# Eight layers on one core: the last layer and the output in steps beside the scan, dt and dt x written once

## The chip, the core and the metric

The kernel runs on one core of a Trainium2 chip. The core has four engines that work side by side: PE (TensorE, the matmuls), DVE (VectorE), ACT (ScalarE) and POOL (GpSimd). SP (SyncE) issues nearly all transfers between DRAM and the on-chip memory. Each engine has its own queue of instructions and takes them strictly in order; an instruction whose input is not ready holds up everything behind it in the same queue. The on-chip memory has two parts: SBUF for data and PSUM, into which PE writes.

The metric is the time of one execution on the device in microseconds (us). The time before is the median of three runs. The profile is of one further execution of the same program.

## The reference

Eight layers, each added to its input `x` (8 sequences, 512 positions, 128 channels, float32), with a layer norm ahead of each. The first six, two attentions with their feed-forward layers, a banded attention and an expert layer, are hardly touched. The seventh is a selective scan with a gated feed-forward behind it; the eighth counts spikes. Cut to what matters:

```python
def L3_attn(x):                      # 16 heads of 8 channels, 48 states
    u  = rmsnorm(x) * norm1_w
    xh = depthwise_conv4(u) @ pw_w.T + pw_b
    dt_x, B, C = split(xh @ x_proj_w.T)              # per head
    dt = softplus(dt_x @ dt_proj_w.T + dt_proj_b)
    h  = exp(dt * A) * h + (dt * xh) * B             # for each position in turn
    y  = sum over states of h * C
    x1 = x + y @ out_proj_w.T + out_proj_b
    h2 = rmsnorm(x1) * norm2_w
    return x1 + (silu(h2 @ gate_w.T) * (h2 @ up_w.T)) @ down_w.T

def L3_ffn(x):
    y = square(relu(x @ W_fc.T)) @ W_proj.T
    mem = 0; count = 0
    for 5 steps:
        mem   = 0.9 * mem + y - (mem > 1)
        count = count + (mem > 1)
    return count / 5

x = x + L3_attn(layer_norm(x))
x = x + L3_ffn(layer_norm(x))
```

The norm of `rmsnorm` is over the 128 channels, and so is the layer norm's.

## The kernel before

The 8 sequences lie in SBUF for the whole run as `X[b]`, four row tiles of 128 positions each (C = 4, 32 row tiles in all). Three functions run one after the other: `l0_l2_attn` (the first five layers, from 0 to about 1000 us), `l2_ffn_l3_attn` (L1138: the expert layer and the scan layer) and `l3_ffn` (L1625: the last layer). After them eight transfers write `X[b]` to the output (L1664). The weights of all layers are loaded into one pool of SBUF, `const`, and stay there.

The code is written as Python loops over tiles of pools. A framework turns each tile that is used again into waits between the engines; the order of instructions on each engine is the order in which the program issues them. A pool gives each name a number of buffers (`bufs`); a tile whose buffers are all taken makes its next writer wait for the last reader. PSUM tiles named `mm` have two buffers and serve all side work of this stage; `bx` has two, `Z` one. The decays have four, `h` six, `gx` and `dr` two, `xk` three.

**Statistics.** `stats` (L199) takes mean and variance of the four tiles of a sequence on DVE. The scan layer's input is normalised from `mv3`: `rstd_of` on DVE (L1177) and POOL (L1178, a power of -0.5), then four subtract-and-multiply on DVE (L1183). The last layer's input is normalised from `mv4` with `begin` and `normalised` (L220, after a square root on ACT for all sequences at once). `flipped` transposes four tiles on PE (L228) and copies them out on ACT (L231, or L233 with a scale).

**prepare(b)** (L1273) computes what the scan of one sequence needs. It is a generator; each `yield` ends a step, 11 in all: norm (on DVE), the scale `rr` and `u` on POOL, transposition (L233), the convolution as four matmuls over shifted input with weights `wk` (L1296; `wk` is built once on POOL, L1234), a matmul that turns the rows (L1301), one for dt (L1305), ACT's abs, exp and relu, then a polynomial for log(1 + z) on POOL in 128x512 pieces (L1315 to L1325). At its end it writes `dt` to DRAM with every row 16 times (4 MB) and `du` = dt times x with every row 8 times (2 MB).

**The scan stage.** The loop runs over b (8), q (4 blocks of 32 channels), g (3 blocks of 16 states) and j (2 halves), 192 pieces. One piece is: `bx`, four matmuls of `gx` with the weights `wb` (L1588); the decay `a`, one exp on ACT with `nA` as scale (L1594); the scan on DVE over 128 x 1024 (L1599), which reads `a` from SBUF and `bx` from PSUM and writes `h`. A group is the two pieces of one (b, q, g). After both pieces of a group the program issues:

- `give()` (L1493) for the group before: 8 matmuls `Z` of `h` with `wc` (L1501), which add up over g; with the last g, `zx` = Z times `xk` on DVE (L1509), and after the last q the generator `rest(b)` joins the list `side`.
- with g = 0 the transfers `fetch` of the next block (L1466 to L1484): four for `xk`, which spread the block's 32 rows of `xh` over 128, one for `gx` (512 KB, from `du_d`), two for `dr` (1 MB together, from `dt_d`). All are issued by SP, in this order.
- with g = 2 `products` of the next block: `gx` times `xk` on POOL (L1488).
- `step(side)`: every generator in `side` goes one step on.

`prepare(b + 2)` joins `side` when the scan of b begins; `prepare(0)` and `prepare(1)` run beside the expert layer (L1421 to L1444). So the side work stands on each engine between the instructions of the scan, in this order:

```python
for g in range(G):
    for j in range(2):
        ...
    late.append((b, q, g, hs, xk))
    if len(late) > 1:
        give()
    if after[0] < NB:
        if g == 0:
            fetch(*after)
        elif g == G - 1:
            products(*after)
    step(side)
```

**rest(b)** (L1514, 9 steps, two of them empty) ends the layer of one sequence: the sum over k (L1520) and a copy (L1525), the output projection (L1530) and the add on DVE (L1531), squares on ACT (L1622), the norm (L1535 on DVE, L1536 and L1538 on POOL), the residual on POOL (L1541), the transposition, two gate matmuls with Silu (L1550, L1552), two up matmuls with a product on DVE (L1557, L1558), the down projection (L1563), the add on DVE (L1567) and the statistics `mv4`.

**The last layer** (L1625) loops over the sequences: norm on DVE, transposition, four matmuls with `f3_fc` (L1635), relu on ACT (L1636), the square on POOL (L1637), 16 matmuls with `f3_pr` (L1641), -y on ACT (L1646). Then the five spike steps on DVE, kept as n = -mem: the first count (L1648), and four times t = 0.9 n - y (L1652), the reset (L1654) and the count (L1655); at the end 0.2 times the count is added to x (L1658). All its buffers are double.

## Time and profile before

| | us |
|---|---|
| median of three runs | 2018.02 (2016.74 to 2020.12) |
| the profiled execution | 2007.65 |
| its span, first to last instruction | 2005.9 |
| first five layers | 0 to about 1000 |
| expert layer, with `prepare` of two sequences beside it | about 1000 to 1277.5 |
| scans, with the rest of each layer beside them | 1277.5 to 1865.5 |
| rest of the last sequence's scan layer | 1865.5 to about 1892 |
| last layer and output | about 1892 to 2005.9 |

Busy time in a stretch is the sum of an engine's instructions in it. PEclk is the share of the full clock that PE was granted; the mean over the span is 0.853. "Idle before" of a group is the time its engine stood still just ahead of it, and the name behind the arrow is what ended it. The groups of the last layer (line, engine, operation, out<-in, shapes, count, busy us, mean ns, idle before and its releaser), from a view of the trace by line from 1865 us to the end:

```profile
L1637 POOL TENSOR_TENSOR h<-h 128x512 f32<-128x512 f32 x32 | 46.9, 1493 | 57.8 <-ACT h L1636 57.8
L1641 PE MATMUL o<-L_ffn_W_proj,h 128*128 128x128 f32 x256 | 41.0, 312 | 16.9 <-POOL h L1637 16.9
L1635 PE MATMUL mm<-xT,L_ffn_W_fc 128*128 128x512 f32 x64 | 30.8, 618 | 0.0
L1655 DVE SCALAR_TENSOR_TENSOR cnt<-n,cnt 128x512 f32<-128x512 f32 x32 | 26.7, 834 | 0.4
L1652 DVE SCALAR_TENSOR_TENSOR t<-n,ny 128x512 f32<-128x512 f32 x24 | 21.4, 894 | 0.0
L1654 DVE SCALAR_TENSOR_TENSOR n<-n,t 128x512 f32<-128x512 f32 x24 | 19.6, 815 | 0.2
L1636 ACT ACTIVATE h<-mm 128x512 f32<-128x512 f32 x32 | 19.1, 597 | 11.7 <-PE mm L1635 11.7
```

DVE has the most to do there, with the recurrence and the counts. The transfers of the stage around the scan, from the page (out<-in, count, KB each, median us from issue to landing):

```profile
dt_d<-dt SPq DMA_DIRECT2D x8, 4096.0 KB, 13.0
dr<-dt_d SPq DMA_DIRECT2D x64, 512.0 KB, 7.9
du_d<-du SPq DMA_DIRECT2D x8, 2048.0 KB, 14.0
gx<-du_d SPq DMA_DIRECT2D x32, 512.0 KB, 6.5
xk<-xh SPq DMA_DIRECT2D x128, 64.0 KB, 6.1
```

### The profile page before, as it was taken

The page shows a single profiled execution, that of the slowest core. Times are in us where ns is not written, and L with a number is a line of the kernel's source. Part 1 is how long each engine was busy: PE and PEld are TensorE (multiplying, and loading weights), DVE is VectorE, ACT ScalarE, POOL GpSimd, SP SyncE. Part 2 cuts the span into 40 slices and gives each one's busy share as a digit, 9 for nine tenths or more (in the row PEclk, how much of TensorE's full clock was granted, in tenths as well). Part 3 has the DMA queues.
Part 4 walks back from the last instruction along what each step waited for, and adds up shares of the span by engine and source line. Part 5 has one row for each costly group of instructions (what it writes and reads, how often), then busy time and mean ns, then how long its engine had stood idle before and what let it go on. Part 6 is the DMA issues. An engine that isn't in the chain of part 4 may idle for free.

```text
span 2005.9 us, 24650 instructions
## 1 busy us (share of the span) xinstructions
PE 1661.1 (83%) x9157; PEld 688.7 (34%) x9157; DVE 1283.0 (64%) x2369; ACT 826.5 (41%) x1197; POOL 655.8 (33%) x708
## 2 busy tenths in 40 slices
PE   6978988999989775785999999698768788698774
PEld 2322333434444363554434444112112112122353
DVE  5656666566655422454565554498878779798489
ACT  4645555544534221442323343345445346345221
POOL 5544433432211204303020054516245244211152
PEclk8989989888999997776999999758778778677788
DMA  8970000000000272000000024653864855842000
GB/s 277 383 222 1 1 1 11 17 10 9 21 16 17 88 223 61 18 1 0 1 0 1 0 79 173 193 156 107 227 192 92 246 169 131 236 111 74 1 16 27
DMA packets 118345, 181.02 MB, mean 90 GB/s; under 512 B 11464, under 2 KB 43088, under 8 KB 118224
## 3 DMA queue, kind: packets, MB, share of 16 engines
q1 hardware_dynamic: 116176, 175.24, 29.4%
q0 software_dynamic: 2048, 4.20, 0.7%
q8 instruction: 72, 1.18, 0.2%
q14 instruction: 49, 0.40, 0.1%
HBM read 74.55 MB, written 96.47 MB: 85 GB/s over the span
## 4 chain that ended last, share of the span: by engine, by line
PE 24%; DVE 14%; issue 5%; DMA 4%; POOL 4%; ACT 1%; SPq 1%; DVEq 0%; POOLq 0%; ACTq 0%
DVE h L1599 5%; PE bx L1588 5%; PE mm L1432 4%; PE acc L1421 4%; DMA dr<-dt_d 3%; PE Z L1501 3%; PE sp L1443 1%; POOL h L1637 1%; DMA gx<-du_d 1%; PE o L1641 1%; DVE act L1444 1%; DVE t L1652 1%; PE mm L1520 1%; SPq L1472 1%; DVE n L1654 1%
## 5 line engine op out<-in xcount | busy, mean ns | idle before, releaser
L1599 DVE TENSOR_TENSOR_SCAN h<-a,bx 128x1024 f32<-128x1024 f32 x192 | 427.9, 2270 | 98.4 <-ACT a L1594 53.0
L1594 ACT ACTIVATE a<-dr,nA 128x1022 f32<-128x1022 f32 x192 | 216.6, 1144 | 308.4 <-DVE h L1599 191.7
L1588 PE MATMUL bx<-gx,wb 32*64 32x512 f32 x1536 | 233.8, 814 | 94.0 <-DVE h L1599 55.1
L1444 DVE TENSOR_TENSOR act<-act,sp 128x512 f32<-128x512 f32 x128 | 87.6, 686 | 128.7 <-ACT act L1436 84.1
L1488 POOL TENSOR_TENSOR gx<-gx,xk 128x1024 f32<-128x1024 f32 x32 | 75.3, 2353 | 253.5 <-DMA gx<-du_d 222.4
L1501 PE MATMUL Z<-h,wc 64*32 64x512 f32 x1536 | 147.5, 830 | 10.5 <-DVE zx L1509 10.3
L1436 ACT ACTIVATE act<-mm 128x512 f32<-128x512 f32 x128 | 76.2, 597 | 164.7 <-PE mm L1432 155.7
L1421 PE MATMUL acc<-act,L_ffn_values 128*128 128x512 f32 x256 | 132.9, 602 | 8.2 <-DVE act L1444 8.1
L1432 PE MATMUL mm<-xT,L_ffn_keys 128*128 128x512 f32 x256 | 135.3, 610 | 0.0
L1588 PEld LDWEIGHTS bx<-gx,wb 32*64 32x64 f32 x1536 | 42.2, 159 | 260.3 <-DVE h L1599 182.5
L470 DVE TENSOR_REDUCE mx<-sm 128x8 f32<-128x1024 f32 x64 | 76.2, 1212 | 46.8 <-POOL sm L466 46.8
L498 POOL TENSOR_SCALAR_AFFINE_SELECT eT<-eT 128x1024 f32<-128x1024 f32 x64 | 68.6, 1095 | 105.6 <-ACT eT L496 105.5
L466 POOL TENSOR_SCALAR_AFFINE_SELECT sm<-sm 128x1024 f32<-128x1024 f32 x64 | 69.3, 1096 | 56.7 <-ACT sm L465 56.3
L496 ACT ACTIVATE eT<-sT 128x1024 f32<-128x1024 f32 x64 | 62.0, 1020 | 57.9 <-PE sT L489 57.8
L465 ACT COPY sm<-sc 128x1024 f32<-128x1024 f32 x64 | 63.0, 1013 | 51.3 <-PE sc L459 31.6
L1178 POOL TENSOR_TENSOR rstd<-rstd,minus_half 128x4 f32<-128x4 f32 x16 | 16.5, 1036 | 192.0 <-DVE rstd L1177 191.9
L459 PE MATMUL sc<-kb,qT 32*128 32x512 f32 x256 | 58.4, 736 | 22.4 <-ACT eT L496 10.2
L321 DVE SCALAR_TENSOR_TENSOR xn<-x,mv,rstd 128x128 f32<-128x128 f32 x128 | 45.9, 409 | 44.5 <-POOL rstd L317 44.4
L1421 PEld LDWEIGHTS acc<-act,L_ffn_values 128*128 128x128 f32 x256 | 47.1, 192 | 65.2 <-issue 46.5
L489 PE MATMUL sT<-qT,kb 32*128 32x512 f32 x256 | 57.1, 692 | 14.2 <-ACT sm L465 8.3
L1432 PEld LDWEIGHTS mm<-xT,L_ffn_keys 128*128 128x128 f32 x256 | 46.2, 192 | 65.2 <-issue 52.1
L199 DVE BATCH_NORM_STATS2 bn<-x 128x6 f32<-128x128 f32 x256 | 64.2, 271 | 6.5 <-DMA x<-in_L_attn_hidden_states 5.4
(411 smaller groups left out, 3203.9 us busy)
## 6 DMA issues: line engine op xcount, KB each, us to landing
f_in<-we SPq DMA_DIRECT2D x10, 3584.0 KB, 27.2
dt_d<-dt SPq DMA_DIRECT2D x8, 4096.0 KB, 13.0
dr<-dt_d SPq DMA_DIRECT2D x64, 512.0 KB, 7.9
du_d<-du SPq DMA_DIRECT2D x8, 2048.0 KB, 14.0
gx<-du_d SPq DMA_DIRECT2D x32, 512.0 KB, 6.5
wt<-in_L_ffn_experts SPq DMA_DIRECT2D x48, 192.0 KB, 2.8
xk<-xh SPq DMA_DIRECT2D x128, 64.0 KB, 6.1
xg<-f_in SPq DMA_DIRECT2D x48, 64.0 KB, 2.6
```

The costliest lines, as they stand in the source:

```text
L466: nc.gpsimd.affine_select(out=sm, in_=sm, compare_op=ALU.is_ge, fill=-1e30, base=0, pattern=[[0, 8], [-1, P]], channel_multiplier=1,)
L470: nc.vector.tensor_reduce(mx[:, c, 2 * i : 2 * i + 2, 0:4], sm.rearrange("p (q r) k -> p q r k", q=2), AX.X, ALU.max, negate=True,)
L498: nc.gpsimd.affine_select(out=e4, in_=e4, compare_op=ALU.is_ge, fill=0.0, base=0, pattern=[[0, 8], [1, P]], channel_multiplier=-1,)
L1421: nc.tensor.matmul(acc, f2_v[:, j, :], act, start=(j == 0), stop=(j == J - 1))
L1432: nc.tensor.matmul(mm, f2_k[:, 2 * j : 2 * j + 2, :], xT, start=True, stop=True)
L1436: nc.scalar.activation(act, mm, AF.Relu)
L1444: nc.vector.tensor_tensor(act, act, sp[j % 4], ALU.mult)
L1488: nc.gpsimd.tensor_tensor(gx, gx, xk.unsqueeze(1).to_broadcast([P, 2, S]), ALU.mult)
L1501: nc.tensor.matmul(zs[q][32 * j : 32 * j + 32, i, :], wc[half, g, :], hs[j // 2][half, j % 2, :], start=(g == 0), stop=(g == G - 1),)
L1588: nc.tensor.matmul(bx[64 * i : 64 * i + 64, k, :], wb[at, g, :], gx[at, i, :], start=True, stop=True,)
L1594: nc.scalar.activation(a[:, :, 1:], dr[:, 2 * j : 2 * j + 2, 1:], AF.Exp, scale=nA[:, q, g : g + 1],)
L1599: nc.vector.tensor_tensor_scan(h.rearrange("p r t -> p (r t)"), a.rearrange("p r t -> p (r t)"), bx.rearrange("p r t -> p (r t)"), 0.0, AL ...
```

## The change

- The last layer is no longer a function of its own. A generator `spikes(b)` of 18 steps does it for one sequence, and joins `side` when `rest(b)` has taken its statistics. Its norm runs on POOL (`normal_aside`), its square on ACT, the count of spikes on POOL, in single buffers and with the PSUM tiles `mm`; it ends with the sequence's output transfer.
- `prepare` also takes its norm on POOL, splits the convolution in two halves and has 14 steps. `rest` has 13 (further steps behind the projection's add, each gate, each up and the last add), and its small scale `r2` goes from DVE to POOL.
- `dt_d` holds dt once (256 KB, written by four transfers), `du_d` holds du once (256 KB). The repetition is in the reads: `gx` comes in two transfers, `dr` in two as before, each from a source that repeats its rows. `gx` is now fetched ahead of `xk`.
- In the scan loop `give` follows the first piece of a group, `fetch` the first piece of a block, `products` the fourth; the side work takes a step after every piece. If the rows of the next sequence aren't ready at a fetch, the side work is driven on until they are.
- Weights of the first layers go to a pool `early` that is closed ahead of the expert layer.

The loads of the other small weights of the first layers move from `const` to `early` in the same way, and the helpers `inv_sqrt`, `begin`, `normalised` and `norm_flip`, which the last layer alone used, are gone.

```diff
+    first_weights = ExitStack()
+    early = first_weights.enter_context(tc.tile_pool(name="early", bufs=1))
...
-    def l2_ffn_l3_attn():
+    def l2_ffn_to_l3():
...
+            def normal_aside(b, mv, r, xn):
+                nc.gpsimd.tensor_scalar(r, mv[:, tiles(b), 1], 1e-5, None, ALU.add)
+                nc.gpsimd.tensor_tensor(r, r, half_T, ALU.pow)
+                for c in range(C):
+                    nc.gpsimd.tensor_scalar(
                         xn[:, c, :], X[b][:, c, :], mv[:, b * C + c, 0:1], r[:, c : c + 1],
                         ALU.subtract, ALU.mult,
                     )
...
-                r = rstd_of(mv3, b)
+                r = work.tile([P, C], F32, tag="rstd", name="rstd", bufs=3)
+                xn = work.tile([P, C, D], F32, tag="x1", name="x1", bufs=4)
+                normal_aside(b, mv3, r, xn)
                 rr = work.tile([P, C], F32, tag="rr", name="rr")
                 nc.gpsimd.tensor_tensor(rr, r, r, ALU.mult)
                 nc.gpsimd.tensor_tensor(rr, rr, mv3[:, tiles(b), 1], ALU.mult)
                 nc.gpsimd.tensor_scalar(rr, rr, 1e-6, None, ALU.add)
-                nc.gpsimd.tensor_tensor(rr, rr, minus_half[:, 0:C], ALU.pow)
-                xn = work.tile([P, C, D], F32, tag="x1", name="x1", bufs=4)
-                normal(b, mv3, r, xn)
+                nc.gpsimd.tensor_tensor(rr, rr, half_T, ALU.pow)
                 x1[b] = xn
...
-                mm = mm_tile()
-                for k in range(4):
-                    nc.tensor.matmul(mm, wk[:, k], up[:, k : k + S], start=(k == 0), stop=(k == 3))
                 xh = work.tile([P, S], F32, tag="xh", name="xh", bufs=3)
-                nc.scalar.activation(xh, mm, AF.Identity, bias=xb)
-                yield True
+                for h in range(0, S, S // 2):
+                    mm = mm_tile()[:, 0 : S // 2]
+                    for k in range(4):
+                        nc.tensor.matmul(
+                            mm, wk[:, k], up[:, h + k : h + k + S // 2], start=(k == 0), stop=(k == 3)
+                        )
+                    nc.scalar.activation(xh[:, h : h + S // 2], mm, AF.Identity, bias=xb)
+                    yield True
                 mm = mm_tile()
                 nc.tensor.matmul(mm, turn, xh, start=True, stop=True)
                 xt = work.tile([P, S], F32, tag="xt", name="xt", bufs=1)
                 nc.scalar.copy(xt, mm)
+                yield True
                 mm = mm_tile()
...
-                dt_d = dram.tile([P, 16, S], F32, tag="dt_d", name="dt_d", bufs=3)
-                nc.sync.dma_start(dt_d, dt.unsqueeze(1).to_broadcast([P, 16, S]))
                 du = work.tile([P, S], F32, tag="du", name="du")
                 nc.gpsimd.tensor_tensor(du, dt, xt, ALU.mult)
-                du_d = dram.tile([P, HD, S], F32, tag="du_d", name="du_d", bufs=3)
-                nc.sync.dma_start(du_d, du.unsqueeze(1).to_broadcast([P, HD, S]))
+                yield True
+                dt_d = dram.tile([2 * Q, 4, 4, S], F32, tag="dt_d", name="dt_d", bufs=3)
+                for r in range(4):
+                    nc.sync.dma_start(dt_d[:, r], dt[r :: 4])
+                du_d = dram.tile([P, S], F32, tag="du_d", name="du_d", bufs=3)
+                nc.sync.dma_start(du_d, du)
                 rows[b] = xh, dt_d, du_d
...
                     of = slice(32 * q, 32 * q + 32)
+                    gx = scan.tile([P, 2, S], F32, tag="gx", name="gx")
+                    for i in range(2):
+                        nc.sync.dma_start(
+                            gx[:, i, :],
+                            du_d[32 * q + 16 * i : 32 * q + 16 * i + 16]
+                            .unsqueeze(1).to_broadcast([16, HD, S]),
+                        )
                     xk = scan.tile([P, S], F32, tag="xk", name="xk", bufs=3)
                     for i in range(4):
                         nc.sync.dma_start(xk[32 * i : 32 * i + 32], xh[of])
-                    gx = scan.tile([P, 2, S], F32, tag="gx", name="gx")
-                    nc.sync.dma_start(
-                        gx, du_d[of].rearrange("m k t -> (m k) t").rearrange("(i p) t -> p i t", i=2)
-                    )
                     dr = scan.tile([P, 4, S], F32, tag="dr", name="dr")
                     for i in range(2):
                         nc.sync.dma_start(
                             dr[64 * i : 64 * i + 64],
-                            dt_d[32 * q + 16 * i : 32 * q + 16 * i + 16]
-                            .rearrange("m s t -> (m s) t").rearrange("(j p) t -> p j t", j=4),
+                            dt_d[2 * q + i].rearrange("r j t -> r (j t)")
+                            .unsqueeze(1).to_broadcast([4, 16, 4 * S]),
                         )
                     rows4[b, q] = xk, gx, dr
...
                     nc.vector.tensor_tensor(xn, xn, pr, ALU.add)
+                    yield True
                     square_sums(xn, ss, b, scan)
                     yield True
                     t = tiles(b)
-                    nc.vector.tensor_scalar(r2[:, t], ss[:, t], 1.0 / D, 1e-6, ALU.mult, ALU.add)
-                    nc.gpsimd.tensor_tensor(r2[:, t], r2[:, t], minus_half[:, 0:C], ALU.pow)
+                    nc.gpsimd.tensor_scalar(r2[:, t], ss[:, t], 1.0 / D, 1e-6, ALU.mult, ALU.add)
+                    nc.gpsimd.tensor_tensor(r2[:, t], r2[:, t], half_T, ALU.pow)
...
                     nc.vector.tensor_tensor(X[b], X[b], o, ALU.add)
+                    yield True
                     stats(b, mv4)
+                    side.append(spikes(b))
+                    yield True
+                def spikes(b):
+                    r = work.tile([P, C], F32, tag="rstd", name="rstd", bufs=3)
+                    xn = scan.tile([P, C, D], F32, tag="u2", name="xn3", bufs=1)
+                    normal_aside(b, mv4, r, xn)
+                    yield True
+                    xT = scan.tile([P, S], F32, tag="hT", name="hT3", bufs=1)
+                    flipped(xn, mm_four(), xT)
+                    yield True
+                    h = scan.tile([P, 4, S], F32, tag="h3", name="h3", bufs=1)
+                    for k in range(4):
+                        mm = mm_tile()
+                        nc.tensor.matmul(mm, f3_fc[:, cols(k)], xT, start=True, stop=True)
+                        nc.scalar.activation(h[:, k, :], mm, AF.Relu)
+                        nc.scalar.activation(h[:, k, :], h[:, k, :], AF.Square)
+                        yield True
+                    ny = scan.tile([P, C, D], F32, tag="ny", name="ny", bufs=1)
+                    for c in range(C):
+                        o = mm_tile()[:, 0:D]
+                        for k in range(4):
+                            nc.tensor.matmul(
+                                o, h[:, k, cols(c)], f3_pr[:, k, :], start=(k == 0), stop=(k == 3)
+                            )
+                        nc.scalar.activation(ny[:, c, :], o, AF.Copy, scale=-1.0)
+                        yield True
+                    ny = ny.rearrange("p c d -> p (c d)")
+                    cnt = scan.tile([P, S], F32, tag="cnt", name="cnt", bufs=1)
+                    nc.gpsimd.tensor_scalar(cnt, ny, -1.0, None, ALU.is_lt)
+                    n = ny
+                    for _ in range(4):
+                        t = scan.tile([P, S], F32, tag="t3", name="t3", bufs=1)
+                        nc.vector.scalar_tensor_tensor(t, n, 0.9, ny, ALU.mult, ALU.add)
+                        n2 = scan.tile([P, S], F32, tag="n3", name="n3")
+                        nc.vector.scalar_tensor_tensor(n2, n, -1.0, t, ALU.is_lt, ALU.add)
+                        n = n2
+                        yield True
+                        hit = scan.tile([P, S], F32, tag="hit", name="hit", bufs=1)
+                        nc.gpsimd.tensor_scalar(hit, n, -1.0, None, ALU.is_lt)
+                        nc.gpsimd.tensor_tensor(cnt, cnt, hit, ALU.add)
+                    yield True
+                    yield True
+                    xf = X[b].rearrange("p c d -> p (c d)")
+                    nc.vector.scalar_tensor_tensor(xf, cnt, 0.2, xf, ALU.mult, ALU.add)
+                    yield True
+                    nc.sync.dma_start(out[b].rearrange("(c p) d -> p c d", p=P), X[b])
                     yield True
...
                                 hs.append(h)
+                                if j == 0 and late:
+                                    give()
+                                if after[0] < NB and (g, j) == (0, 0):
+                                    while after[0] not in rows:
+                                        step(side)
+                                    fetch(*after)
+                                elif after[0] < NB and (g, j) == (1, 1):
+                                    products(*after)
+                                step(side)
                             late.append((b, q, g, hs, xk))
-                            if len(late) > 1:
-                                give()
-                            if after[0] < NB:
-                                if g == 0:
-                                    fetch(*after)
-                                elif g == G - 1:
-                                    products(*after)
-                            step(side)
                 give()
                 while side:
                     step(side)
-            state["mv"] = mv4
...
-    def l3_ffn():
-        with ExitStack() as es:
...
-    for layer in (l0_l2_attn, l2_ffn_l3_attn, l3_ffn):
-        layer()
-    for b in range(NB):
-        nc.sync.dma_start(out[b].rearrange("(c p) d -> p c d", p=P), X[b])
+    l0_l2_attn()
+    first_weights.close()
+    l2_ffn_to_l3()
```

## The prediction

> **What bounds the kernel now.** I first cut the span at the first and last state scan (L1599 runs from 1277.5 to 1863.3 us) with busy times by stretch; everything the change touches lies after 1277.5 us.
>
> ```profile
> core 0: us, PE busy (x) PEld busy (x) DVE busy (x) ACT busy (x) POOL busy (x), PEclk, DMA share, GB/s
> 1277.50:1865.50 588.00, 477.76 (x3492) 113.51 (x3492) 492.27 (x331) 272.25 (x319) 214.68 (x172) 0.74 0.59 160
> 1865.50:2005.90 140.40, 90.54 (x416) 57.59 (x412) 101.34 (x160) 35.20 (x63) 50.21 (x35) 0.84 0.05 16
> ```
>
> The scan stage takes 588.0 us, of which DVE works 492.3 and stands still for 95.7. Behind it come 140.4 us without any scan: the rest of sequence 7's layer (to about 1890) and the whole last layer with the output. Next the waits inside the scan stage (who, for whom, total us, times, longest):
>
> ```profile
> POOL gx L1488 <- DMA gx<-du_d: 220.6, 20, 17.1
> ...
> ACT a L1594 <- DMA dr<-dt_d: 116.4, 11, 19.0
> ...
> DVE h L1599 <- ACT a L1594: 53.0, 7, 11.4
> ...
> DVE h L1599 <- PE bx L1588: 44.3, 31, 5.5
> PE bx L1588 <- POOL gx L1488: 37.0, 6, 9.2
> ```
>
> Of DVE's idle time 53.0 us end with a decay `a`, which itself waited for the read of dt; 44.3 us end with the input `bx`, and part of that is PE waiting for `gx` (37.0), which waited for a transfer too. The costs of one piece of work, from the page:
>
> ```profile
> L1599 DVE TENSOR_TENSOR_SCAN h<-a,bx 128x1024 f32<-128x1024 f32 x192 | 427.9, 2270 | 98.4 <-ACT a L1594 53.0
> ...
> L1588 PE MATMUL bx<-gx,wb 32*64 32x512 f32 x1536 | 233.8, 814 | 94.0 <-DVE h L1599 55.1
> ...
> L1501 PE MATMUL Z<-h,wc 64*32 64x512 f32 x1536 | 147.5, 830 | 10.5 <-DVE zx L1509 10.3
> ```
>
> Last, stretches of one kind: 1306 to 1342, where PE has only bx and Z, and five stretches with side work and few transfers.
>
> ```profile
> 1306.00:1342.00 36.00, 36.00 (x223) 5.78 (x224) 32.49 (x16) 15.52 (x14) 4.71 (x2) 0.50 0.59 163
> ...
> 1345.00:1402.00 57.00, 46.70 (x384) 13.65 (x372) 49.95 (x40) 30.31 (x39) 33.36 (x31) 0.91 0.38 98
> 1426.00:1474.00 48.00, 42.34 (x344) 12.48 (x340) 44.44 (x36) 27.09 (x36) 29.71 (x28) 0.92 0.44 99
> 1510.00:1558.00 48.00, 39.11 (x312) 12.22 (x308) 39.64 (x34) 27.37 (x36) 28.45 (x25) 0.89 0.38 96
> 1582.00:1630.00 48.00, 41.19 (x320) 12.54 (x324) 40.50 (x27) 27.01 (x36) 27.33 (x24) 0.87 0.44 100
> 1666.00:1714.00 48.00, 41.29 (x344) 12.45 (x340) 46.25 (x34) 29.38 (x38) 26.14 (x22) 0.96 0.41 105
> ```
>
> Without side work the clock is 0.50 and PE is full; with it the clock is 0.87 to 0.96 and DVE is busy 220.8 of 249 us, 89%. So with transfers out of the way the stage is DVE's, with PE close behind.
>
> [...] both bx of a group back to back took 1.11 us at 1386.95, one alone 1.09 at 1390.93. [...] L1652 took 0.89 us on average beside POOL and 0.68 at the end, where POOL was done. The scan reads one input from PSUM and stays at 2.25 to 2.29.
>
> **The change, part by part.**
>
> *Last layer moved (`spikes`).* The stage of 114 us behind 1892 goes. Sequences 0 to 6 do this work beside later scans; 7 does it alone at the end. Tail now: 24.6 us from the last scan's end (1865.5) to mv4 (1890.1). That chain stays. Then `spikes(7)`: on POOL 0.2 + 1.03 (L1536) + 4 x 0.60 (the nearest row, the 128x128 tensor_scalar of L1234, 603 ns) = 3.7; flip 1.1 + copy 0.6; first fc 1.0 and eight ACT passes of 0.60 = 5.8; 16 proj pairs 3.2 (L1641) + last copy 0.5; POOL's count 0.6 + four times (0.62 + 1.27) + first t and n 1.4 = 9.6, slower than DVE's 4 x 1.4; last add 0.7; store and end 3.7 (1x 2002.2 to 2005.9); a dozen hand-overs of 0.1, 1.2. Sum 31. Tail after: 24.6 + 31 = 56 (50 to 64). Gain 140.4 - 56 = **84 us**.
>
> *What it adds to the scan stage.* On DVE per sequence: t and n, 4 x (0.89 + 0.81) = 6.8, last add 0.7: 7.5, the old count (L1655) being on POOL. Seven sequences 52, of which about 4 fall into the tail: +49. Removed: L1183 4.8, L1535 4.8 and L1177 0.2 go to POOL: -10. DVE work 492 + 49 - 10 = **531 us**. PE per sequence: flip 0.9, fc 8 instructions 3.9, proj 4.1 to 5.1: about 9. ACT: 0.6 + 8 x 0.6 + 4 x 0.3 and one more pair of table loads, 2 x 1.28, because Silu now has an exp between its halves: 9 per sequence; ACT had 272 of 588, so it is covered. POOL: 3.7 + 8.2 for spikes, 3.7 and 0.2 moved from DVE: some 16 per sequence, to about 330 of 590, also covered; if it lags, the last add on DVE waits, and every scan behind it. Bounded at 0 to 3 us a sequence, taken 0.5, because two empty steps lie before it.
>
> *dt and dt x once in DRAM.* Writes fall from 6 MB to 0.5 MB per sequence, the reads stay at 7 MB. The dt read is issued behind 2 + 4 other transfers, about 5 us, and lands after 4.7 us (the fastest now) to 7.9 (the median): 10 to 13 us after the fetch starts. The fetch now begins at the first half of group 0, so it has five half groups, 15 us. The waits of 53.0 and about 30 of the 44.3 us fall to some 5 each. Whether sixteen readers of one DRAM row are slower no row shows: 0 to 3 us at each of 32 fetches; I take 0, half a group being free. SP's new entries (five small stores, one output) stand behind a fetch, six half steps before the next, so a wait for POOL there delays no fetch; 10 us of it would eat the slack.
>
> *Steps twice as often.* The built order of matmuls is now bx0(n), Z(n-1), side, bx1(n), side. Before, bx0 and bx1 stood together, and Z and side followed. Two costs: the pair no longer merges (1.09 each against 1.11 for both at full clock: +1.1 us a group), and bx1(n), which needs scan1(n-1), now has Z's second half and a side step ahead of it. The loop scan1(n-1), half Z 0.5 to 1.0, side about 1, bx1 1.1, hand-overs 0.2, scan1(n) 2.27 is 5.1 to 5.6 us. DVE's own work per group is 531/96 = 5.5. PE: 2 x 1.1 + 1.1 + side. Side per sequence is 18.6 (16 L1520 1.9, L1296 3.7, L1301 and L1305 2, two flips 1.1, L1530 1.1, gates and ups 4, L1563 2, rounded up for spill) + 9 = 27, 2.3 per group: 5.6. Three loops of nearly one length hold each other up, so DVE won't be busy all the time.
>
> *The rest* (halves of the convolution, small weights in a region that is freed, L2 stage): same work, the order of the stages before 1277 us hardly moves: 0, -3 to +3.
>
> *Sum.* DVE busy share in the stage: 89% in the side-laden stretches, which still hold some transfer waits; the tighter order takes that gain back. 531/0.89 = 597 us. 588 to 597: +9. Total +9 - 84 = -75 us. The profiled execution took 2007.65 (span 2005.9, 1.75 around it) and lies 10.4 below the median of 2018.02; on it 1933, on the median **1943 us**.
>
> **The rivals.**
> *A, DVE truly full:* with no transfer waits and a warm clock DVE gets 95% (it had 96% from 1666 to 1714). Stage 559, -29 - 84: 1905. For it: the loop estimates fit within 5.5. Against: bx apart.
> *B, the reads still come late:* sixteen-fold reads of one row, or fetches queued behind stores: half of the 53 + 30 us stays. Stage 597 + 40, total -35: 1983. For it: 7 MB per sequence still go through, and the dt read is last in its fetch.
> *C, slower: PE at half clock becomes the bound.* Place: the matmuls between the scans, L1588 and L1501. Cold, a group costs 2 x 1.98 + 1.96 + 2 x 2.3 = 10.5 us against 5.6 warm. To eat 84 us the stage must reach 672, 7.0 per group: a cold share of 28%. Now the share is 52% over the stage (0.74), 8 to 26% in the side-laden stretches. At 35% a group takes 7.3 us, the stage 702, the end +30: 2048. [...] Against: almost every step now brings full-array matmuls.
> *D, the move costs what it saves* (order of instructions as said, gain eaten by waits for POOL, two PSUM tiles for three side jobs): within 5 us of 2018.
>
> **How the numbers follow.** About 0.2%, 4 us, is what can be told from no change. Forecast (1920 to 1965) 0.56, A 0.14, B 0.15, C 0.12, D 0.03. Faster: forecast, A and B, 0.85; same 0.03; slower 0.12. Range: down to A's 1905 less the unknown ends of tail and first part, 1900; up past B to 2000, which leaves C and a little of A outside.
>
> **What would show it.** Right: scans end near 1875, behind them about 56 us; the wait of `a` for dr under 15 us in all; the clock over 0.85 in the stage; DVE busy near 530 in it. Wrong: clock at 0.75 or less with PE full (C); dr and gx landing later than 8 us (B); DVE waiting for POOL's cnt; a stage before 1277 that moved.

## The result and the profile after

The changed kernel takes 2142.31 us (median of four runs, 2136.32 to 2155.56), the kernel before beside it 2018.87 us. The ratio is 1.062 with a 95% interval of 1.057 to 1.068: slower by 6%, where 1943 us was forecast. The profiled execution took 2137.55 us, its span is 2135.8.

The busy times by stretch, cut at the first and last scan (now L1646), from the same view as before:

```profile
core 0: us, PE busy (x) PEld busy (x) DVE busy (x) ACT busy (x) POOL busy (x), PEclk, DMA share, GB/s
1296.00:2069.50 773.50, 623.26 (x3842) 178.85 (x3842) 546.10 (x365) 338.71 (x430) 341.52 (x298) 0.79 0.30 79
2069.50:2135.80 66.30, 27.41 (x102) 13.86 (x102) 19.68 (x29) 11.33 (x26) 32.09 (x26) 0.69 0.03 8
```

The end did shrink, from 140.4 us to 66.3. But the first scan starts at 1296.3 instead of 1277.5 us, 19 later, and the stage of the scans takes 773.5 us instead of 588.0, 185 longer. DVE's work there grew by only 54 us. Who waits for whom in that stage (total us, times, longest):

```profile
DVE h L1646 <- PE bx L1635: 196.6, 70, 14.0
POOL gx L1484 <- DMA gx<-du_d: 146.5, 16, 21.7
...
POOL gx L1484 <- DMA xk<-xh: 85.6, 8, 20.8
...
PE mm L209 <- POOL xn L1169: 63.6, 28, 10.0
...
ACT a L1641 <- DMA dr<-dt_d: 42.0, 8, 14.5
...
DVE h L1646 <- ACT a L1641: 24.3, 2, 23.1
```

The costs of a piece, from the page (columns as before):

```profile
L1646 DVE TENSOR_TENSOR_SCAN h<-a,bx 128x1024 f32<-128x1024 f32 x192 | 433.7, 2277 | 225.8 <-PE bx L1635 196.6
...
L1635 PE MATMUL bx<-gx,wb 32*64 32x512 f32 x1536 | 240.7, 728 | 40.6 <-DVE h L1646 27.6
L1497 PE MATMUL Z<-h,wc 64*32 64x512 f32 x1536 | 171.4, 737 | 42.7 <-DVE h L1646 42.6
```

A scan costs what it did (2277 ns), `bx` and Z together 412 us of PE instead of 381; what more than doubled is DVE's idle time ahead of a scan, 225.8 us after 98.4. DVE now waits 196.6 us for `bx` (44.3 before). A wait that wasn't there before is PE's, 63.6 us, in front of the transpositions (L209) of the last layer's norm, which POOL makes (L1169). One sequence in the timeline shows how these hang together (start, duration, engine, instruction, in brackets the idle time before it and its releaser):

```profile
1619.34 2.25 SPq L1465 DMA_DIRECT2D gx<-du_d  x2
...
1624.80 2.34 POOL L1484 TENSOR_TENSOR gx<-gx,xk 128x1024 f32<-128x1024 f32 x1 [7.22 <-DMA gx<-du_d]
1627.22 0.42 POOL L1166 TENSOR_SCALAR rstd<-mv 128x4 f32<-128x4 f32 x2
1627.61 2.02 POOL L1167 TENSOR_TENSOR rstd<-rstd,minus_half 128x4 f32<-128x4 f32 x2
1629.62 3.13 POOL L1169 TENSOR_SCALAR xn<-x,mv,rstd 128x128 f32<-128x128 f32 x4
1630.48 0.47 PE L209 MATMUL mm<-ident,xn 128*128 128x128 f32 x1 [8.70 <-POOL xn L1169]
...
1633.21 1.99 PE L1635 MATMUL bx<-gx,wb 32*64 32x512 f32 x8
...
1635.33 2.29 DVE L1646 TENSOR_TENSOR_SCAN h<-a,bx 128x1024 f32<-128x1024 f32 x1 [12.49 <-PE bx L1635]
```

POOL stands 7.2 us at a product whose `gx` is still on its way. The norm, whose input is ready, is queued behind it; PE stands 8.7 us at the transposition of that norm; `bx` is queued behind that on PE, and DVE stands 12.5 us. Then PE is back at half clock: the granted clock was 1.00 from 1612 to 1618 us, where a `bx` took 1.09 us (at 1617.41), and 0.50 from 1624.8 to 1648, so that this `bx` takes 1.99. And the start of the stage:

```profile
1275.11 1.22 SPq L1475 DMA_DIRECT2D dr<-dt_d  x2
...
1295.09 5.31 ACT L1641 ACTIVATE a<-dr,nA 128x1022 f32<-128x1022 f32 x5 [14.48 <-DMA dr<-dt_d]
```

The first read of `dr` is issued at 1275.1, and the first decay, which waits for it, starts at 1295.1. In between the DMA engines are mostly idle. Two stretches of that wait (columns as in the first block of this section), the second with little but the reads of `dr` in it:

```profile
1281.00:1295.00 14.00, 0.00 (x0) 0.00 (x0) 0.00 (x0) 0.00 (x0) 13.01 (x14) 0.57 0.37 86
1284.00:1293.00 9.00, 0.00 (x0) 0.00 (x0) 0.00 (x0) 0.00 (x0) 8.37 (x9) 0.50 0.25 73
```

A share of 0.25 is what 4 of the 16 DMA engines make if they are always busy, or all 16 if they are busy a quarter of the time; the view gives their mean alone.

One sentence of the section on the kernel has to be corrected here: the order on an engine is not simply that in which the program issues. The framework plans it, with its own idea of when data will be ready. In the trace of the changed kernel DVE does two steps `t`, `n`, `t` of the recurrence in a row (1664.86 to 1667.2 us), where the program puts a scan after each pair. So an experiment that changes the program may change the order elsewhere too; below it is said where the order was kept, and the traces agree.

### The profile page after: what moved, and what is told of

It reads as the page before. It is cut to its first block, busy times and chain, and to the rows that moved or that the text cites. A ratio compares the mean times of both kernels' runs of the same rounds, so it can differ in the third digit from the quotient of the medians.

```text
span 2135.8 us, 24951 instructions
## 1 busy us (share of the span) xinstructions
PE 1750.0 (82%) x9221; PEld 718.4 (34%) x9221; DVE 1251.7 (59%) x2248; ACT 870.4 (41%) x1273; POOL 782.1 (37%) x844
## 3 DMA queue, kind: packets, MB, share of 16 engines
q0 software_dynamic: 2048, 4.20, 0.6%
## 5 line engine op out<-in xcount | busy, mean ns | idle before, releaser
L1646 DVE TENSOR_TENSOR_SCAN h<-a,bx 128x1024 f32<-128x1024 f32 x192 | 433.7, 2277 | 225.8 <-PE bx L1635 196.6
L1635 PE MATMUL bx<-gx,wb 32*64 32x512 f32 x1536 | 240.7, 728 | 40.6 <-DVE h L1646 27.6
L1497 PE MATMUL Z<-h,wc 64*32 64x512 f32 x1536 | 171.4, 737 | 42.7 <-DVE h L1646 42.6
L209 PE MATMUL mm<-ident,xn 128*128 128x128 f32 x192 | 46.9, 354 | 105.0 <-POOL xn L1169 69.0
L1497 PEld LDWEIGHTS Z<-h,wc 64*32 64x32 f32 x1536 | 26.2, 114 | 177.3 <-issue 86.5
L433 PE MATMUL sc<-kb,qT 32*128 32x512 f32 x256 | 58.4, 747 | 24.5 <-ACT eT L470 10.2
L209 PEld LDWEIGHTS mm<-ident,xn 128*128 128x128 f32 x192 | 27.6, 164 | 136.9 <-POOL xn L1169 83.7
L968 POOL DMA_INDIRECT back<-f_out,back_at x32 | 31.7, 990 | 104.8 <-issue 104.3
```

What stands on the lines that cost most here:

```text
L209: nc.tensor.transpose(ps[:, c, :], src[:, c, :], ident)
L1497: nc.tensor.matmul(zs[q][32 * j : 32 * j + 32, i, :], wc[half, g, :], hs[j // 2][half, j % 2, :], start=(g == 0), stop=(g == G - 1),)
L1635: nc.tensor.matmul(bx[64 * i : 64 * i + 64, k, :], wb[at, g, :], gx[at, i, :], start=True, stop=True,)
L1646: nc.vector.tensor_tensor_scan(h.rearrange("p r t -> p (r t)"), a.rearrange("p r t -> p (r t)"), bx.rearrange("p r t -> p (r t)"), 0.0, AL ...
```

## The experiments

Times are medians; the ratio is to runs of the kernel before on the same chip, with its interval. "Old transfers" are those of the kernel before (dt written 16 times, dt x 8 times, reads without repetition).

### Which part costs: first four

Three empty steps between the last layer's norm and its transposition.

```diff
                     normal_aside(b, mv4, r, xn)
                     yield True
+                    yield True
+                    yield True
+                    yield True
```

> Three empty steps are put between the last layer's norm on POOL and its transposition on PE; nothing else changes. Theory T1 (POOL's queue): PE stands 63.6 us in front of transpositions that wait for a norm which stands on POOL behind the product of gx, itself waiting for its transfer, and PE comes back at half clock; then the stage loses 60 to 110 us: 2035 to 2080 us. Theory T2 (bx apart, so PE's order makes one long loop over the scan): less than 20 us, 2120 to 2142. Theory T3 (slow reads of dt and dt x): no change, 2130 to 2145.

2119.18 us, 1.051 (1.044 to 1.059). PE's wait for the norm fell from 69.0 to 20.6 us (from the start of the stage to the end of the program), but its wait in front of Z rose from 42.6 to 72.9 us and DVE's for POOL's count from 23.2 to 48.8. 23 us came back, a part of T1 at most, and not a clean test: the order on all four engines is another, so the steps shifted other work too.

Both `bx` of a group together.

```diff
                             for j in range(2):
                                 bx = ps3.tile([P, 2, S], F32, tag="bx", name="bx")
+                                bxs.append(bx)
...
+                            for j in range(2):
+                                bx = bxs[j]
                                 a = decays[n % 4]
```

> The matmuls bx of both pieces of a group stand together again, ahead of Z and of both side steps; all else is as in the changed kernel. T2: the loop from a scan over Z and a side step to the next bx is gone, a group falls from 8.04 towards 6.5 us (PE's own work): 150 us less, about 1990, at the least 60 less. T1: the stalls for POOL stay and only the second bx of the group is ahead of them: 2110 to 2140. T3: no change.

2184.75 us, 1.087 (1.081 to 1.093). T2 falls: with `bx` paired the kernel is slower still. PE now waits 89.9 us in front of `bx` for a scan to free its buffer, with Z and the side work queued behind. The order on the other engines moved a little too; a later run that pairs `bx` by taking the old loop order (2112 instead of 2013) goes the same way.

The read of `dr` in four transfers of 16 partitions.

```diff
-                        nc.sync.dma_start(
-                            dr[64 * i : 64 * i + 64],
-                            dt_d[2 * q + i].rearrange("r j t -> r (j t)")
-                            .unsqueeze(1).to_broadcast([4, 16, 4 * S]),
-                        )
+                        for r in range(4):
+                            at = 64 * i + 16 * r
+                            nc.sync.dma_start(
+                                dr[at : at + 16],
+                                dt_d[2 * q + i, r].rearrange("j t -> (j t)")
+                                .unsqueeze(0).to_broadcast([16, 4 * S]),
+                            )
```

> Each read of dr is cut into four transfers of 16 partitions, so that its outermost dimension is 16 and not 4; same bytes. T3: the read took some 15 us at about 70 GB/s, as if only a few of the DMA engines carried it; the first scan starts about 15 us earlier than 1296 and gx comes sooner, in all 20 to 60 us less: 2080 to 2120. T1 and T2: only the start gains, 10 to 19 us: 2120 to 2132.

2295.71 us, 1.144 (1.137 to 1.150): a miss for all theories. The first scan does start at 1276.5, 20 us earlier. About half of that is an earlier fetch: the first read of `dr` is issued at 1264.6 instead of 1275.1. The other half is the read itself, 10.7 us from issue to the first decay instead of 20.0, with each row still read by 16 partitions, and now with the DMA engines busy:

```profile
1264.60:1272.00 7.40, 4.14 (x25) 1.48 (x23) 0.00 (x0) 2.84 (x5) 4.15 (x5) 1.00 0.94 142
```

But the planner built another order of the side work: long runs of it stand between groups of scans, and the stage takes 951.6 us, so the total says nothing of the reads. That there are eight transfers in place of two can't alone be why: a kernel below has eight as well and keeps the changed kernel's order.

The old transfers in the changed kernel.

> dt and dt x are written 16 and 8 times to DRAM again and read as in the kernel before; steps, loop and last layer are those of the changed kernel. T3: the changed reads cost 20 to 60 us, so 2080 to 2120. T1: gx lands later behind the large writes, the stalls for POOL grow: 2140 to 2200. T2: within 15 us of 2125, only the start gains.

2013.24 us, 1.001 (0.998 to 1.003). All of the loss is gone, more than any theory gave. PE, DVE and ACT have exactly the changed kernel's order here, so the 129 us hang on the transfers and what they bring with them. For POOL's order differs in five places: five products of `gx` stand behind a norm instead of ahead of it. The stage and PE's waits of this kernel:

```profile
1279.80:1941.00 661.20, 566.49 (x3842) 169.21 (x3842) 545.52 (x365) 336.56 (x429) 352.01 (x307) 0.88 0.52 145
```

```profile
PE mm L209 <- POOL xn L1169: 6.3, 6, 4.5
```

PE's wait for the norm is 6.3 us instead of 69.0. So two causes are mixed: when the data come, and what POOL has queued behind the product.

### Taking the two causes apart

Only dt as before, dt x still written once and spread by its read.

```diff
-                dt_d = dram.tile([2 * Q, 4, 4, S], F32, tag="dt_d", name="dt_d", bufs=3)
-                for r in range(4):
-                    nc.sync.dma_start(dt_d[:, r], dt[r :: 4])
+                dt_d = dram.tile([P, 16, S], F32, tag="dt_d", name="dt_d", bufs=3)
+                nc.sync.dma_start(dt_d, dt.unsqueeze(1).to_broadcast([P, 16, S]))
```

> The changed kernel with dt written 16 times and read as before, while dt x stays written once and spread by its read; same order on PE, DVE and ACT. T3a (the read of dr alone is slow, since its outermost dimension is 4): nearly all of the 130 us that the old transfers gave come back, 2010 to 2040. T3b (every spreading read is slow): gx still comes late and POOL's products with it, 2060 to 2110.

2015.98 us, 1.002 (1.000 to 1.004): T3a. The eightfold read of dt x (16 rows outermost) is harmless; the loss hangs on dt. This kernel too has the five products behind the norms.

The changed transfers alone, in the kernel before.

> The kernel before with nothing changed but the transfers: dt and dt x written once and spread by the reads, as in the changed kernel; the order of instructions on PE, DVE and ACT is that of the kernel before. T3 (the spreading reads are slow: 1 MB of dr at some 70 GB/s is 14 us, against 18.4 us that a block of three groups now takes): the waits of the decays for dr and of the products for gx grow, 60 to 140 us more than before: 2075 to 2155. T4 (the reads hurt only beside the longer side work of the changed kernel): within 20 us of before, 2000 to 2035.

2087.54 us, 1.038 (1.035 to 1.040): T3. Here no last layer stands beside the scans, and the order of PE, DVE and ACT is that of before. POOL's differs in a few products; a later run (the wide reads in the kernel before, 0.995) has the same POOL order, so the 4.3% between the two come from the transfers alone. These differ in the width of the read of dt, and with it in how often a row is repeated (4 times instead of 16), in the number of reads and in 1 MB instead of 256 KB written.

Dt written four times by 16 stores, the read 16 rows wide.

```diff
-                dt_d = dram.tile([2 * Q, 4, 4, S], F32, tag="dt_d", name="dt_d", bufs=3)
-                for r in range(4):
-                    nc.sync.dma_start(dt_d[:, r], dt[r :: 4])
+                dt_d = dram.tile([2 * Q, 16, 4, S], F32, tag="dt_d", name="dt_d", bufs=3)
+                for r in range(16):
+                    nc.sync.dma_start(dt_d[:, r], dt[r // 4 :: 4])
...
-                            .unsqueeze(1).to_broadcast([4, 16, 4 * S]),
+                            .unsqueeze(1).to_broadcast([16, 4, 4 * S]),
```

> The changed kernel with dt written 4 times (16 stores, 1 MB) instead of once, and each row spread 4 times by its read instead of 16 times; so the read of dr has 16 as its outermost dimension and not 4; still two transfers a block, and the order on PE, DVE and ACT is the changed kernel's. T3c [...]: the DMA share during that read goes from about 0.25 to 0.9, the decays stop waiting, and most of the 126 us come back: 2010 to 2045. T3d (spreading one row is slow in itself, however wide): half or less comes back, 2080 to 2130.

2065.23 us, 1.028 (1.024 to 1.032): 77 us come back, of the 126 that the old dt gave. Between the two theories: the DMA share around the first read is 0.5 to 0.9 (1265 to 1272 us in slices of 1 us, other reads included), the first scan starts at 1273.3 us, the decays hardly wait, but PE still stands 39.3 us for the norm, since POOL's order is the changed kernel's.

The same with one store of 1 MB, and eight reads of a block.

```diff
+                dt_d = dram.tile([P, 4, S], F32, tag="dt_d", name="dt_d", bufs=3)
+                nc.sync.dma_start(dt_d, dt.unsqueeze(1).to_broadcast([P, 4, S]))
...
+                        for j in range(4):
+                            m = 32 * q + 16 * i + 4 * j
+                            nc.sync.dma_start(
+                                dr[64 * i : 64 * i + 64, j, :],
+                                dt_d[m : m + 4].rearrange("m v t -> (m v) t")
+                                .unsqueeze(1).to_broadcast([16, 4, S]),
+                            )
```

> The changed kernel with dt written 4 times by one store of 1 MB, and read by 8 transfers a block, each with 16 rows outermost and spread 4 times; order on PE, DVE, ACT and POOL as in the changed kernel. T3c (the 4 outermost rows were the fault, and in the run with 16 stores these stood ahead of the reads): as with the old transfers, 2000 to 2030. T3d (a spreading read is slow however wide): 2050 to 2100.

2076.77 us, 1.034 (1.027 to 1.040), in the range of T3d, but not for its reason: these reads land 2.5 us after their issue at the least and 4.4 at the most (before: 4.7 to 14.2, each of them four times as large). PE still waits 35.2 us for the norm. Left is POOL's order, which the next two runs change alone: seven products move behind a norm.

Products queued behind the norm, with the changed kernel's transfers and with the wide ones.

```diff
-                    nc.gpsimd.tensor_scalar(
+                    state["norm"] = nc.gpsimd.tensor_scalar(
                         xn[:, c, :], X[b][:, c, :], mv[:, b * C + c, 0:1], r[:, c : c + 1],
...
-                    nc.gpsimd.tensor_tensor(gx, gx, xk.unsqueeze(1).to_broadcast([P, 2, S]), ALU.mult)
+                    with tc.issue_after(state["norm"].ins):
+                        nc.gpsimd.tensor_tensor(gx, gx, xk.unsqueeze(1).to_broadcast([P, 2, S]), ALU.mult)
```

> The changed kernel with one thing else: each product of gx is queued on POOL behind the last norm issued ahead of it in the program; the order on PE, DVE, ACT and SP is untouched. T1' (PE waits 69 us for norms that stand behind a product waiting for its transfer, and comes back at half clock): 40 to 70 us less than 2142: 2072 to 2102. T11 (the slow read of dr holds the loop anyway, so PE would wait elsewhere, as three empty steps showed, which gave 23 us): 2115 to 2145.

> The same queueing of the products in the kernel with dt written 4 times by one store and read 16 rows wide. T1': the 60 us that this kernel was above the one with the old transfers go, 2000 to 2030. T3d (spreading reads cost in themselves): 2060 to 2085.

With the narrow reads 2062.57 us, 1.024 (1.021 to 1.028), 80 us less than the changed kernel and 10 us better than the best case of T1'. With the wide reads 2011.49 us, 0.999 (0.997 to 1.001), 65 us less and as T1' expected. In the timeline of POOL in the first of them the norm stands ahead of the product, and waits for nothing:

```profile
1593.23 0.42 POOL L1166 TENSOR_SCALAR rstd<-mv 128x4 f32<-128x4 f32 x2
1593.62 2.02 POOL L1167 TENSOR_TENSOR rstd<-rstd,minus_half 128x4 f32<-128x4 f32 x2
1595.63 3.15 POOL L1169 TENSOR_SCALAR xn<-x,mv,rstd 128x128 f32<-128x128 f32 x4
1601.03 2.35 POOL L1485 TENSOR_TENSOR gx<-gx,xk 128x1024 f32<-128x1024 f32 x1 [2.26 <-DMA xk<-xh]
```

The order of PE, DVE and ACT is the same in all four kernels of this table (ratio to before), so the loss of 131 us can be divided. The read of dt is worth 65 us with the product ahead of the norm and 51 behind it, POOL's order 80 us with the narrow read and 65 with the wide one:

| | product ahead of the norm | behind it |
|---|---|---|
| read of dt 4 rows wide | 1.062 (changed kernel) | 1.024 |
| read of dt 16 rows wide | 1.034 | 0.999 |

Two ends stay open. The wide read also repeats each row 4 times instead of 16; width with 16 readers kept was seen at the start of the stage only, in the run with four transfers of 16 partitions. And behind the norm the narrow read shows itself as 12 us more of DVE's waits in front of decays (24.5 against 12.7) and 35 in front of `bx` (124.7 against 89.9); how a read of `dr` delays `bx` was not followed.

### Why the rest is only level with before

With the old transfers: the loop order of the kernel before in the changed kernel.

```diff
-                                if j == 0 and late:
-                                    give()
...
-                                step(side)
                             late.append((b, q, g, hs, xk))
+                            if len(late) > 1:
+                                give()
...
+                            step(side)
+                            step(side)
```

> The changed kernel with the old transfers and the loop order of the kernel before: both pieces of a group, then Z, the transfers and two side steps. T5 (steps between the two pieces put Z and side work ahead of the second bx, which DVE then waits for: 97.5 us with the old transfers): 30 to 70 us less than the 2013 of the kernel with the old transfers: 1945 to 1985. T6 (PE and DVE simply have that much more to do, wherever it stands): within 15 us of 2013.

2112.06 us, 1.050 (1.048 to 1.052): the opposite of T5. Then the changed loop and steps, with the last layer at the end as before; and the reverse, the last layer beside the scans with the loop, steps and transfers of before.

> The changed kernel with the old transfers and the last layer and the outputs at the end as in the kernel before: what is left of the change is the shorter steps, twice as often, Z after the first piece, and the norms on POOL. T5' (the finer order serves the scans): the stage of the scans falls from 588 towards 530 us, total 1945 to 1980. T6 (PE and DVE have the same work, so it gives nothing): 2005 to 2025. T2 (bx apart costs): 2040 to 2080.

> The kernel before with only the move: the last layer and the output as steps beside the scans, one step a group, with the loop, steps and transfers of the kernel before. T6 (what the move adds to PE and DVE in the stage, some 70 us, nearly equals the 75 us that the end loses, whatever the steps): 2000 to 2035. T5 (it takes the finer steps to fit the last layer in): 2060 to 2110, as slow as the kernel with the old loop order was.

The finer steps alone give 2010.40 us, 0.999 (0.997 to 1.001): T6. The move alone gives 2064.34 us, 1.025 (1.021 to 1.029): T5, as slow as expected of it. Their stages of the scans, in this order:

```profile
1292.90:1881.00 588.10, 501.75 (x3532) 125.10 (x3532) 488.99 (x307) 295.55 (x338) 228.56 (x195) 0.90 0.57 160
```

```profile
1281.40:1998.00 716.60, 538.57 (x3758) 159.02 (x3762) 550.75 (x388) 310.71 (x399) 339.93 (x278) 0.76 0.47 134
```

The finer steps leave the stage at 588 us though the clock is 0.90 instead of 0.74 (this profiled execution was the longest of its 13, 2023.34 us). The move with coarse steps costs 129 us there, with fine steps (the kernel with the old transfers) 73, and the end is 73 and 75 shorter.

Two tries at the loop's own waits: Z one group later, then the same with four buffers of `xk`; and four buffers of `xk` alone.

```diff
-                                if j == 0 and late:
+                                if j == 0 and len(late) > 1:
                                     give()
```

> The changed kernel with the old transfers, and Z one group later, so that it no longer waits for the scan just ahead of it. T5: PE's 36.9 us in front of Z go and the loop scan, Z, side, bx is cut: 30 to 60 us less than 2013: 1955 to 1985. T6: within 15 us of 2013.

> The changed kernel with the old transfers and Z one group later, this time with four buffers of xk instead of three; same order as the run with the late Z. T7 (the late Z kept xk, so that the next fetch, whose first transfer writes xk, started a group later): the 73 us that the late Z cost go and the wait of Z goes too: 1975 to 2015. T8 (the loss lay in the order, not in xk): 2070 to 2090.

> The changed kernel with the old transfers and four buffers of xk instead of three; same order. T7 (SP stood 137 us in front of xk, waiting for zx to free it, with the reads of gx and dr behind): 10 to 30 us less than 2013: 1985 to 2005. T6 (gx and dr are in time as it is, PE's and DVE's work sets the pace): within 10 us of 2013.

2085.66 us, 1.034 (1.028 to 1.040); 2085.49 us, 1.040 (1.033 to 1.046); 2011.77 us, 1.002 (1.000 to 1.004). The late Z no longer waits for a scan, yet DVE waits 158.4 and 124.7 us for `bx`, against 97.5 with the old transfers alone, at clocks of 0.73 and 0.78 in the stage instead of 0.88. The order differs from the kernel with the old transfers on all four engines, so the cause stays open. The second of these kernels ran from 2051.5 to 2102.6 us, and its trace is of the shortest execution; none of the four is in the range of T7. With Z in its old place more `xk` gives nothing (T6).

The wide reads in the kernel before.

> The kernel before, its steps and loop unchanged, with the transfers of the last run: dt written 4 times by one store, dt x once, all reads 16 rows wide. Before, DVE waited 53 us for decays and PE 37 us for gx, both behind 6 MB of writes a sequence; now these are 1.25 MB. T10 (the writes made those reads late): half or more of it goes, 1950 to 1990. T3d: no gain, 2005 to 2060.

1997.85 us, 0.995 (0.993 to 0.997): a gain of some 10 us, between the ranges of T10 and T3d. DVE's 53.0 us for decays are gone, while its wait for `bx` rose from 44.3 to 77.9, at a PE clock of 0.75 (0.74 before).

Last, the spikes counted on DVE, as before the change, in the kernel with wide reads and products behind the norms.

```diff
-                    nc.gpsimd.tensor_scalar(cnt, ny, -1.0, None, ALU.is_lt)
+                    nc.vector.tensor_scalar(cnt, ny, -1.0, None, ALU.is_lt)
...
-                        nc.gpsimd.tensor_scalar(hit, n, -1.0, None, ALU.is_lt)
-                        nc.gpsimd.tensor_tensor(cnt, cnt, hit, ALU.add)
+                        nc.vector.scalar_tensor_tensor(cnt, n, -1.0, cnt, ALU.is_lt, ALU.add)
```

> The last kernel (dt written 4 times, reads 16 rows wide, products behind the norms) with the spikes counted on DVE as in the kernel before; POOL loses the counts, 2 operations of 1.5 and 1.3 us four times a sequence. T12 (counts on POOL stretch t and n on DVE and end last): DVE's 4 x (1.16 + 1.17) become 4 x (0.7 + 0.7 + 0.7), the wait for the count (15 us in all) goes, the end is 5 to 7 us shorter: 1980 to 2003. T6 (PE's order and clock set the pace): 2003 to 2020.

1983.08 us, 0.988 (0.984 to 0.991): in the range of T12, 1.2% below the kernel before. The recurrence in the stage of the scans (line, engine, operation, count, busy us, mean ns), first with the counts on POOL, then with all on DVE:

```profile
L1606 DVE SCALAR_TENSOR_TENSOR n<-n,t 128x512 f32<-128x512 f32 x19 | 22.3, 1173 | 0.6
L1604 DVE SCALAR_TENSOR_TENSOR t<-n,ny 128x512 f32<-128x512 f32 x19 | 22.0, 1158 | 0.2
```

```profile
L1609 DVE SCALAR_TENSOR_TENSOR cnt<-n,cnt 128x512 f32<-128x512 f32 x25 | 16.9, 677 | 0.3
L1606 DVE SCALAR_TENSOR_TENSOR n<-n,t 128x512 f32<-128x512 f32 x18 | 12.4, 688 | 0.4
L1604 DVE SCALAR_TENSOR_TENSOR t<-n,ny 128x512 f32<-128x512 f32 x18 | 12.1, 671 | 0.0
```

Three operations of 0.68 us take less of DVE than two of 1.17 beside the counts on POOL. The stage falls from 661.0 to 650.4 us and what follows the last scan from 66.1 to 55.2, about twice the 5 to 7 us that T12 gave.

## Why the prediction was wrong

**The step that failed first** is in "dt and dt x once in DRAM": "Whether sixteen readers of one DRAM row are slower no row shows: 0 to 3 us at each of 32 fetches; I take 0", with a landing 10 to 13 us after the fetch starts. The first read took 20 us from issue to decay, and its fetch had started 4 us earlier. What mattered most, as far as the runs tell, was not the sixteen readers but the shape: four rows outermost. With them the read ran at 73 GB/s with a DMA share of 0.25 (1284 to 1293 us). With 16 partitions outermost and sixteen readers the share was 0.94 at 142 GB/s, other reads included, and the read took 10.7 us from issue to decay. With 16 rows outermost, four readers and two transfers it took about 7.2 (issued at 1264.9, first scan at 1273.3, so the first decay at about 1272.1), so the readers may have cost about the 3 us that the bound allowed. How the shape comes to set the share was not shown. The wide read with four readers gave 65 us back (2142 to 2077). The changed transfers, narrow read included, also slow the kernel before by 3.8% when they are the only change, where the wide ones gain 0.5%. Rival B had the mechanism, late reads, and was priced at 40 us.

**The second** is in "What it adds to the scan stage": "if it lags, the last add on DVE waits, and every scan behind it. Bounded at 0 to 3 us a sequence, taken 0.5". POOL did lag, not for its busy time but because a product that waits for its transfer stands ahead of the norm, and the one that waited was PE, 69 us in all. Taking the products away from there gave 80 us with the narrow reads and 65 with the wide ones. The text had looked for stores behind a fetch on SP, and not for what stands behind a waiting product on POOL. Before, POOL waited 220.6 us in front of the same products, and it cost little: in the stage of the scans no transposition on PE waited for POOL, only `bx` for the products themselves, 37.0 us.

**The third** is the sum for the stage, 531/0.89 = 597. With both faults mended it is 661: DVE works 546 and is busy 82.6%. Of the 64 us too few, 18 are the work, 546 instead of 531: mostly the steps `t` and `n`, taken at 0.89 and 0.81 us and measured at 1.16 and 1.17. The 0.89 was not a price beside POOL but a mean: of the 24 rows of L1652 before, the middle one took 0.68 us and the longest 1.56, and with POOL's counts beside it the middle one of `t` takes 1.43. The other 46 are the share (531/0.826 = 643). The 89% came from stretches in which PE had 0.95 us of work for each of DVE's (210.6 against 220.8); in the mended kernel it has 1.04 (566 against 546). That the loop through Z, side work and `bx` then leaves neither engine full is an argument that no run isolates. So the mended change stands at the number of rival D, which had 0.03: 73 us more in the stage against 75 less at the end. D's reasons, waits for POOL and too few PSUM tiles, were not shown apart.

**The end** was forecast at 56 us and is 66.3. The items of its sum for `spikes(7)` add up to 30.1 and not 31. About half of what was missing is POOL's count: taken at 9.6 us with the first `t` and `n`, it took 14.9 from the last -y to the last add, the first count 2.01 us and the others 1.49 to 1.81 + 1.26 to 1.76 instead of 0.62 + 1.27. The rest is spread: 27.7 instead of 24.6 us from the last scan to the statistics, 17.6 instead of 14.9 from there to the last -y, 6.0 instead of 4.4 for add and store. With the counts on DVE, in the last experiment, the end is 55.2.

**Rival C** gave 2048 for a cold share of 35%. The cold share was 42%, an estimate from the mean clock of 0.79 that takes the clock to be either 0.50 or 1.00, and its own formula gives 7.7 us a group against 8.05 measured. But `bx` apart as the cause of the low clock finds no support: pairing `bx` made the kernel slower (2184.75 us, at a clock of 0.76 in the stage against 0.79), and the clock in the stage rose to 0.88 (old transfers) and 0.89 (wide reads, products behind the norms) when the waits for transfers and the norm went, with `bx` still apart: in these runs a low clock went with the stalls rather than with `bx` apart.

Nearly right were the steps that the stages ahead move little (the first fetch is issued at 1271.3 instead of 1264.3 us, 7 later where 3 was allowed) and that DVE would have some 530 us of work (546). Right was that the decays' waits for `dr` in the running stage don't bind DVE: of DVE's 24.3 us in front of decays 23.1 are the start. Its sign for this, under 15 us of ACT's waits for `dr`, failed all the same: they are 42.0.

## What to carry to other kernels

Before a repetition is moved from the write to the read of a transfer, look at the outermost dimension that is left: here the bytes saved in DRAM were lost again, as the read with 4 rows outermost ran at 73 GB/s with a DMA share of 0.25. When work that another engine waits for is put on an engine that was idle, look through its queue for an instruction that waits for a transfer: here its waiting, 220.6 us before the change, cost little as long as nothing urgent stood behind it, and after the change PE stood 69 us for the norm. And where a planner builds the order, compare the built orders of two versions first, since a change in transfers alone can move instructions elsewhere.

## What the runs showed of the hardware

- The steps `t` and `n` of the recurrence, scalar_tensor_tensor on DVE over 128x512, took 0.67 and 0.69 us on average in the stage of the scans with the counts on DVE, and 1.16 and 1.17 while POOL counted (both with wide reads and products behind the norms). In the changed kernel, where POOL counts too, the shortest `t` took 0.69 us, the middle one 1.43 and the longest 2.67. Why they take longer was not shown.
- Reading one row into 16 partitions kept the DMA engines as busy as reads without repetition and moved less: the run with four transfers of 16 partitions had a share of 0.94 at 142 GB/s (1264.6 to 1272 us), the old transfers a share of 0.94 at 222 GB/s (1268 to 1276 us), other reads included in both. The rows read were also longer (8 KB instead of 2 KB), so how much of this is the repetition stays open.
